# Inner norm moved from VectorE to ScalarE and GpSimd, the last groups normalised in PSUM batch by batch, and a reordered first group, in a two-layer graph kernel

## The chip, the cores and the metric

The kernel runs on one core of one Trainium2 chip. A core has TensorE (PE in the profile; PEld is its weight load), VectorE (DVE), ScalarE (ACT), GpSimd (POOL) and SyncE (SP), which here only issues DMA transfers. The metric is the device time of one execution in microseconds. The time of a version is the median of its runs.

## The reference, cut to what matters

The input x is 128 batches of 128 tokens by 512 features; adj is a 128 x 128 matrix.

```python
A = einsum('od,bdn->bon', adj, x); C = A + b[None, :, None]
pre = A[:, :, None, :] + (C - A)[:, :, :, None]
x = layernorm(x + max(relu(pre), axis=-1))
# layer 1: masked attention with 8 heads, projection, inner norm, residual
q, k, v = split(x @ w_qkv)
attn = softmax(where(adj == 0, -inf, q @ k.T * scale))
o = (attn @ v) @ w_proj + b_proj
ln = (o - mean(o)) * rsqrt(var(o) + 1e-5) * ln_gamma + ln_beta
x = layernorm(x + o + ln)
```

The "inner norm" is `ln`; the outer one is the last line. All data and products are float32.

## The kernel before, in words

**Tiling.** The 128 batches are 32 groups of four. A group passes through layer 0 (`l0_mm`, `l0_stats`, `l0_norm_one`, a transpose through DRAM), then `qk_unit`, `scores`, `softmax`, `v_unit`, `attend`, `o_unit` and `tails`. Three groups are in flight: in turn p of the main loop, group p has its softmax and v, group p+2 its layer 0, group p+1 its q and k, group p-1 its output projection and tail.

**Products.** q and k come from sums of blocks of tokens times 26 ready-made sums of weight blocks (`weight_forms`, tile wqk), with partial results carried between PSUM banks by ScalarE copies into `u` tiles (L777) or other banks (L773). The token sums (`token_sums`, tiles hl) are GpSimd's. v and the output projection use seven products for eight (`Unit`), again with sums on GpSimd.

**First group.** There is no wqk yet, so q and k of group 0 come from plain products (`qk_plain`), which read x1T, transposed on TensorE (`l0_transpose_pe`, L567) and copied from PSUM to SBUF by VectorE (L583). Ahead of that adj is transposed (L422) and copied (L423), layer 0 runs for each batch, and `finish` (L462) makes scale `rs` and shift `sh` on GpSimd for a ScalarE norm (`norm`, L495).

**Tails.** `tails` (L1155) takes statistics of o on VectorE, `rs` on GpSimd (`root_only`, L1144), then two VectorE instructions for each batch: (o - mean) * gamma, then times rs plus o, into z. GpSimd adds z to the reloaded row r (2 batches at once), and a second norm on ScalarE gives the output. z is one buffer for both halves of a group; r lies in xr0 and xr1. r was written to DRAM (`spill`) after GpSimd had added ln_beta to it (`l0_beta_spill`, L591), and only then is the x buffer reloaded for a later group.

**Last groups.** Group 31 has a plain projection for each batch (`project`, L1376). Group 30's tail is `tail_pool` (L1348): a ScalarE norm, then three GpSimd passes. Group 31's is `tail_open` and `tail_close` (L1386, L1406): VectorE as above, with r added in PSUM by a product with the identity. `outer` (L1365) is the second norm and the output.

**Order.** Nothing is issued as the code stands. Each step is `plan.add(engine, cost, emit, reads, writes)`; `Plan.run` (L194) simulates the engines with these costs. TensorE's steps keep their program order. Every other step has a due time worked back from what needs it (`schedule`, L217), and each engine takes the ready step that is due first. A step that nothing needs, such as an output transfer, was due at the end of the whole program plus 9 us. The resulting order is then fixed for every engine and for SP's queue.

Of the kernel before, what the change touches and what calls it, by code (L numbers as in the profile page):

```python
# [135 lines left out]
class Op:  # L136
    __slots__ = ("n", "eng", "cost", "emit", "lag", "kb", "preds", "succs", "due", "start", "done")
# [22 lines left out]
class Plan:  # L160
# [5 lines left out]
    def add(self, eng, cost, emit, reads=(), writes=(), lag=None, kb=0):  # L166
        op = Op(len(self.ops), eng, cost, emit, self.LAG[eng] if lag is None else lag, kb)
        for accesses, writing in ((reads, False), (writes, True)):
# [22 lines left out]
    ROUNDS, KEPT = 4, 0.5  # L191
    SLOWER, LATER = 1.05, 2.0

    def run(self, lead):  # L194
# [10 lines left out]
        for _ in range(self.ROUNDS):  # L205
            order = self.schedule(start)
            last = max(op.done for op in start)
            if best is None or last < best[0]:
                best = last, order
            t = was = lead  # L210
            for op in start:
                t += self.KEPT * (op.start - was)
                was, start[op] = op.done, t
                t += op.cost
        return best[1]

    def schedule(self, ideal):  # L217
        ops = self.ops
        end = max(ideal[op] + op.cost for op in ideal) + 9.0
        for op in reversed(ops):  # L220
            ahead = op.lag + (self.AHEAD_DMA + 1.5 * op.kb / self.KB_PER_US if op.kb else self.AHEAD)
            due = min(
                (s.due - (0.0 if s.eng == op.eng == "PE" else ahead) for s in op.succs),
                default=end,
            )
# [22 lines left out]
        while todo:  # L248
# [16 lines left out]
            op.done = free[e] = now + op.cost * (1.0 if e == "PE" else self.SLOWER)  # L265
# [19 lines left out]
def kernel(  # L285
# [137 lines left out]
    plan.add("DVE", 0.25, lambda: pin(V.tensor_copy(adjT.t, pt0.t[:, :P])), [pt0], [adjT])  # L423
# [33 lines left out]
    def bn(src, reads, mv, c):  # L457
        st = small("st", 6)
        plan.add("DVE", 0.61, lambda: pin(V.bn_stats(st.t, src())), reads, [st])  # L459
        plan.add("DVE", 0.09, lambda: pin(V.bn_aggr(mv.t[:, c], st.t)), [st], [(mv, c)])  # L460
# [33 lines left out]

    def norm(dst, src, stat, reads, writes):  # L495
# [20 lines left out]
    def l0_stats(g):  # L516
        mv = buf(f"mvy{g % 2}", [P, G, 2])
        for j in range(G):
            xb = xs[2 * g + j // 2]
            bn(lambda xb=xb, j=j: xb.t[:, j % 2], [(xb, j % 2)], mv, j)  # L520
# [46 lines left out]
    def l0_transpose_pe(f, k):  # L567
# [5 lines left out]
        def emit():  # L573
            for c in range(KC):
# [4 lines left out]
        plan.add(  # L579
            "DVE",  # L580
            0.61,
            lambda: pin(
                V.tensor_copy(  # L583
                    xT.t[:, h, :, ts(j, P)], b.t.rearrange("p (c n) -> p c n", c=KC)
                )
            ),
            [b],
            [(xT, (h, j))],
        )
# [23 lines left out]
    def weight_forms():  # L613
# [12 lines left out]
        turn = 0  # L626

        def add(dst, dst_at, a, b, sa, sb_):
            nonlocal turn
            (ba, ka, pa), (bb, kb, pb) = a, b  # L630
            reads = [(ba, ka), (bb, kb)]
            if sa < 0 and sb_ < 0:
# [5 lines left out]
                    [dst_at],  # L638
                )
# [4 lines left out]
            turn += 1  # L644
            if turn % 5 < 3:
                plan.add("DVE", 0.62, lambda: tt(V, dst(), pa(), pb(), op), reads, [dst_at])
            else:
                plan.add("POOL", 0.71, lambda: tt(GP, dst(), pa(), pb(), op), reads, [dst_at])
# [38 lines left out]
    def qk_plain(h, banks, eng):  # L687

        xT = x1T_buf(0)
        for n in range(4):  # L690
            b = bank(banks[n])
            for half in range(2):
# [11 lines left out]
                plan.add("PE", 1.725, emit, [raw[n], (xT, (h, 0)), (xT, (h, 1))], [b])  # L704
# [315 lines left out]
    def softmax(b, bs):  # L1020
# [45 lines left out]
        for i in range(H):  # L1066
            plan.add(
                "ACT",
                0.295,
                lambda i=i: pin(  # L1070
                    A.activation(  # L1071
                        flat()[:, i], flat()[:, i], AF.Identity, scale=rec.t[:, i : i + 1]
                    )
                ),
                [rec, (s, i)],
                [(s, i)],
            )
        u = buf(f"pu{b % 2}", [P, Q, H, QS])
# [76 lines left out]
    def tails(g):  # L1155
# [5 lines left out]
        rs = root_only(mv, range(G))  # L1161
        rows = []
        for h in range(2):
# [5 lines left out]
            for j in range(2):  # L1169
                c = 2 * h + j  # L1170
                plan.add(
                    "DVE",
                    0.7,
                    lambda z=z, o=o, j=j, c=c: stt(
                        z.t[:, j], o.t[:, j], mv.t[:, c, 0:1], ga_bc.t, ALU.subtract, ALU.mult
# [308 lines left out]
```

## Time and profile before

| | |
|---|---|
| median of 3 runs | 1913.92 us (1913.4 to 1914.2) |
| profiled execution, its own time | 1916.16 us |
| its span | 1914.4 us |
| granted TensorE clock, mean | 0.994 |
| busy share: PE, DVE, ACT, POOL | 98%, 81%, 73%, 70% |
| mean DMA rate | 179 GB/s |

The span runs from the first to the last instruction of the profiled execution, which is one execution and not the median. Lines of the profile name the line of the code (a helper such as L340, `tt`, or L343, `stt`, stands for many steps, so the tiles tell them apart), the engine, the operation, output and inputs with their shapes. In the list of groups there follow the count, the busy time in us with the mean in ns, and the idle time of the engine ahead of them with what ended it. A matmul of float32 shows as two records.

### The profile page before, as it was taken

Reading aid. Unit: us, or ns where it says so; the run is one execution under the profiler, and the core shown is the slowest. Engines: PE = TensorE matmul, PEld = TensorE weight load, DVE = VectorE, ACT = ScalarE, POOL = GpSimd, SP = SyncE. Lnnn points to the kernel's source line nnn. Section 1 sums busy time; section 2 is a strip of 40 time slices with the busy share of each in tenths; the row PEclk is TensorE's granted clock in tenths of the full one; section 3 lists DMA queues with packets and bytes.
Section 4 is the critical chain, followed back from the end, with each engine's and each line's share of the span. In section 5 each row is a group of like instructions: output and inputs, shape, how many; then the busy total and the mean of one; then the engine's idle time right before and its main releaser. Section 6 shows DMA issues by size and latency. Waiting matters only on the chain.

```text
span 1914.4 us, 35277 instructions
## 1 busy us (share of the span) xinstructions
PE 1876.4 (98%) x11307; PEld 1595.4 (83%) x11307; DVE 1558.2 (81%) x2634; ACT 1405.4 (73%) x4285; POOL 1332.8 (70%) x1454
## 2 busy tenths in 40 slices
PE   9899999999999999999999999999999999999995
PEld 6788888888888888888888888888888888888882
DVE  7678878889788878888788888888788887888774
ACT  2776778777778777778777787776788767787784
POOL 7658667667577767777677767686776776777746
PEclk9999999999999999999999999999999999999998
DMA  6656675566766566765576756676765667666653
GB/s 204 183 130 155 184 204 162 171 168 193 204 188 168 172 179 187 210 178 167 164 194 179 211 164 172 169 200 186 211 144 172 179 188 210 178 170 171 165 193 116
DMA packets 444856, 341.89 MB, mean 179 GB/s; under 512 B 276736, under 2 KB 378240, under 8 KB 444672
## 3 DMA queue, kind: packets, MB, share of 16 engines
q1 hardware_dynamic: 444384, 339.11, 63.7%
q8 instruction: 91, 1.49, 0.3%
q14 instruction: 93, 0.76, 0.1%
q10 hardware_dynamic: 288, 0.52, 0.1%
HBM read 172.82 MB, written 166.72 MB: 177 GB/s over the span
## 4 chain that ended last, share of the span: by engine, by line
PE 91%; DVE 3%; ACT 3%; POOL 1%; issue 1%; DMA 0%; ACTq 0%; DVEq 0%; POOLq 0%
PE k L346 91%; DVE z L343 2%; ACT s L1071 1%; ACT s L1054 1%; POOL x L340 1%; DVE wqk L340 0%; ACT u L777 0%; DVE k L340 0%; POOL rs L340 0%; ACT k L773 0%; DMA x<-in_x_dram 0%; DVE qk L343 0%; ACT x L501 0%; DVE st L459 0%; DVE x1T L583 0%
## 5 line engine op out<-in xcount | busy, mean ns | idle before, releaser
L346 PE MATMUL k<-hl,wqk 128*128 128x256 f32 x2232 | 518.9, 380 | 2.1 <-ACT k L773 2.0
L346 PEld LDWEIGHTS k<-hl,wqk 128*128 128x128 f32 x2232 | 424.4, 190 | 61.2 <-POOL hl L340 2.5
L1054 ACT ACTIVATE s<-s,nm 128x128 f32<-128x128 f32 x1024 | 397.2, 391 | 31.2 <-DVE nm L1045 31.2
L340 POOL TENSOR_TENSOR hl<-x1T 128x512 f32<-128x512 f32 (+1 forms) x250 | 237.8, 961 | 134.3 <-PE k L346 90.2
L1071 ACT ACTIVATE s<-s,rec 128x128 f32<-128x128 f32 x1024 | 325.5, 392 | 0.0
L346 PE MATMUL k<-x1T,wqk 128*128 128x256 f32 x992 | 250.0, 383 | 9.1 <-ACT u L777 5.6
L886 ACT COPY u<-k 128x512 f32<-128x512 f32 x189 | 110.0, 582 | 196.1 <-PE k L346 195.4
L777 ACT COPY u<-k 128x512 f32<-128x512 f32 x341 | 194.2, 584 | 73.2 <-DVE k L340 30.6
L346 PE MATMUL k<-wv,hl 128*128 128x256 f32 x1024 | 241.4, 379 | 0.0
L346 PEld LDWEIGHTS k<-wv,hl 128*128 128x128 f32 x1024 | 194.5, 190 | 52.1 <-issue 21.5
L346 PE MATMUL k<-wp,so 128*128 128x256 f32 x992 | 224.8, 379 | 0.5 <-ACT k L861 0.5
L343 DVE SCALAR_TENSOR_TENSOR s<-k,mask 128x512 f32<-128x512 f32 x256 | 156.2, 683 | 83.0 <-PE k L346 83.0
L346 PEld LDWEIGHTS k<-x1T,wqk 128*128 128x128 f32 x992 | 188.3, 191 | 40.6 <-ACT u L777 11.4
L343 DVE SCALAR_TENSOR_TENSOR qk<-k,u 128x512 f32<-128x512 f32 x248 | 165.4, 682 | 62.9 <-PE k L346 39.9
L346 PEld LDWEIGHTS k<-wp,so 128*128 128x128 f32 x992 | 188.4, 190 | 26.6 <-ACT k L861 0.9
L340 POOL TENSOR_TENSOR hl<-x1T,hl 128x512 f32<-128x512 f32 (+1 forms) x249 | 201.9, 822 | 0.5 <-DMA x1T<-xhop 0.5
L1054 ACT ACTIVATION_READ_ACCUMULATOR s<-s,nm 128x1 f32 x1024 | 194.2, 190 | 0.0
L346 PE MATMUL k<-wv,x1T 128*128 128x256 f32 x768 | 179.5, 383 | 0.0
L340 POOL TENSOR_TENSOR x<-x,be_bc 128x1024 f32<-128x1024 f32 x62 | 153.2, 2470 | 35.1 <-ACT xr L501 16.4
L346 PE MATMUL k<-wp,oT 128*128 128x256 f32 x744 | 170.7, 379 | 0.0
L1083 DVE STREAM_TRANSPOSE pu<-s 128x1024 f32<-128x1024 f32 x128 | 158.1, 1235 | 12.1 <-ACT s L1071 12.0
L1132 ACT COPY oT<-k 128x512 f32<-128x512 f32 x128 | 74.9, 585 | 120.3 <-PE k L346 120.3
(139 smaller groups left out, 3345.1 us busy)
## 6 DMA issues: line engine op xcount, KB each, us to landing
hop<-pu SPq DMA_DIRECT2D x128, 512.0 KB, 2.7
s<-hop SPq DMA_DIRECT2D x512, 128.0 KB, 3.7
spill<-x SPq DMA_DIRECT2D x62, 512.0 KB, 4.3
xhop<-xt SPq DMA_DIRECT2D x248, 128.0 KB, 3.4
x1T<-xhop SPq DMA_DIRECT2D x248, 128.0 KB, 5.0
x<-in_x_dram SPq DMA_DIRECT2D x60, 512.0 KB, 5.9
xr<-spill SPq DMA_DIRECT2D x60, 512.0 KB, 5.4
out_dram<-xr SPq DMA_DIRECT2D x60, 512.0 KB, 4.4
```

The source lines that it names most:

```text
L340: pin(eng.tensor_tensor(dst, a, b, op))
L343: pin(V.scalar_tensor_tensor(dst, a, s, b, op0, op1))
L346: pin(PE.matmul(dst, lhsT=lhsT, rhs=rhs, start=start, stop=True, skip_group_check=True))
L777: plan.add("ACT", 0.5, lambda b=b, u=u: pin(A.copy(u.t, b.t)), [b], [u])
L886: plan.add("ACT", 0.5, lambda: pin(A.copy(u.t, b.t)), [b], [u])
L1054: A.activation(flat()[:, i], flat()[:, i], AF.Exp, bias=nm.t[:, i : i + 1], accum_out=sm.t[:, i : i + 1],)
L1071: A.activation(flat()[:, i], flat()[:, i], AF.Identity, scale=rec.t[:, i : i + 1])
L1083: V.transpose(u.t.rearrange("p q h b -> p h q b"), flat().rearrange("p h (q a) -> p h q a", q=Q),)
L1132: lambda: pin(A.copy(dst.t[:, :, ts(jj, P)], bk.t.rearrange("p (c n) -> p c n", c=KC))),
```

## The change

It has six parts.

1. The planner: a step that nothing needs is due 9 us after the start of the TensorE step ahead of it in the program. Steps marked `both` take VectorE and GpSimd together in the plan. It makes six rounds and not four.
2. First group: the statistics stand behind the copy of adj; `finish_first` makes the shift on VectorE; the copy of x1T is split between VectorE and ScalarE, and a product waits for its half alone; two of the l0 products of group 1 come two plain products later.
3. `weight_forms`: sums that were shared between VectorE and GpSimd are all VectorE's.
4. `softmax`: in group 0 (last two batches) and group 31 (first two) the final scale is one VectorE instruction, not eight ScalarE ones.
5. `tails`: the inner norm is a ScalarE norm and two more GpSimd passes over two batches.
6. Last groups: `tail_before` for group 30 norms into a PSUM bank and then has two VectorE passes, with r + o on GpSimd; `tail` for group 31 works in its PSUM bank. They are called batch by batch between attends and projections; the products with the identity go.

```diff
 class Plan:
+        op.after, op.both = self.pe, both
+        op.preds.update(behind)
-    ROUNDS, KEPT = 4, 0.5
+    ROUNDS, KEPT, BEHIND = 6, 0.5, 9.0
     def schedule(self, ideal):
-        end = max(ideal[op] + op.cost for op in ideal) + 9.0
...
+            if op.succs:
+                due = min(s.due - (0.0 if s.eng == op.eng == "PE" else ahead) for s in op.succs)
+            else:
+                due = ideal.get(op.after, 0.0) + self.BEHIND
...
+            op.done = now + op.cost * (1.0 if e == "PE" else self.SLOWER)
+            if op.both:
+                op.done += max(0.0, free["POOL"] - now)
+                free["POOL"] = op.done
+            free[e] = op.done
+    def finish_first(mv, c, rows):
+        rs, t, sh = small("rs", G), small("st", 6), small("sh", G)
+        def root():
+            pin(GP.tensor_scalar(rs.t[:, :1], mv.t[:, c : c + 1, 1], EPS, None, ALU.add))
+            tt(GP, rs.t[:, :1], rs.t[:, :1], mhalf.t, ALU.pow)
+        plan.add("POOL", 0.85, root, [(mv, c), mhalf], [rs])
+        r = lambda: rows.t[:, c : c + 1]
...
+            lambda: pin(V.tensor_scalar(t.t[:, :1], mv.t[:, c : c + 1, 0], r(), None, ALU.add)),
...
+                V.tensor_scalar(
+                    sh.t[:, :1], r(), t.t[:, :1], rs.t[:, :1], ALU.subtract, ALU.mult
+                )
...
     def l0_stats(g):
-            bn(lambda xb=xb, j=j: xb.t[:, j % 2], [(xb, j % 2)], mv, j)
+            bn(lambda xb=xb, j=j: xb.t[:, j % 2], [(xb, j % 2)], mv, j, [adj_done])
     def l0_transpose_pe(f, k):
+        for half in range(2):
+            at = [(xT, (h, j, half))]
+            if half:
+                plan.add("ACT", 0.4, lambda ops=operands: pin(A.copy(*ops())), [b], at)
+            else:
+                plan.add("DVE", 0.4, lambda ops=operands: pin(V.tensor_copy(*ops())), [b], at)
     def weight_forms():
-            if turn % 5 < 3:
-                plan.add("DVE", 0.62, lambda: tt(V, dst(), pa(), pb(), op), reads, [dst_at])
-            else:
-                plan.add("POOL", 0.71, lambda: tt(GP, dst(), pa(), pb(), op), reads, [dst_at])
+            plan.add("DVE", 0.49, lambda: tt(V, dst(), pa(), pb(), op), reads, [dst_at], both=True)
-    def softmax(b, bs):
+    def softmax(b, bs, on_vector=False):
+        if on_vector:
+                "DVE",
+                1.55,
+                lambda: tt(
+                    V, flat(), flat(), rec.t.unsqueeze(2).to_broadcast([P, H, P]), ALU.mult
+                ),
...
     def tails(g):
-        rs = root_only(mv, range(G))
+        stat = finish(mv, range(G))
...
-                    lambda z=z, o=o, j=j, c=c: stt(
-                        z.t[:, j], o.t[:, j], mv.t[:, c, 0:1], ga_bc.t, ALU.subtract, ALU.mult
-                    ),
...
-                    lambda z=z, o=o, j=j, c=c: stt(
-                        z.t[:, j], z.t[:, j], rs.t[:, c : c + 1], o.t[:, j], ALU.mult, ALU.add
-                    ),
...
+                norm(
+                    lambda z=z, j=j: z.t[:, j],
+                    lambda o=o, j=j: o.t[:, j],
+                    stat[2 * h + j],
+                    [o],
+                    [(z, j)],
                 )
+            plan.add(
+                "POOL",
+                2.34,
+                lambda z=z: tt(GP, z.t, z.t, ga_bc.t.unsqueeze(1).to_broadcast([P, 2, D]), ALU.mult),
+                [z, ga_bc],
+                [z],
+            )
+            plan.add("POOL", 2.34, lambda z=z, o=o: tt(GP, z.t, z.t, o.t, ALU.add), [z, o], [z])
             plan.add("POOL", 2.34, lambda z=z, r=r: tt(GP, r.t, r.t, z.t, ALU.add), [z, r], [r])
...
-        (s,) = finish(mv0, [c], rcol[0])
-        l0_norm_one(0, c, s)
+        l0_norm_one(0, c, finish_first(mv0, c, rcol[0]))
...
-    for f, k in zip(range(4, 8), (0, 1, 2, 3)):
-        l0_mm(f, k)
+    for f in (4, 5):
+        l0_mm(f, f - 4)
...
+    qk_plain(1, (4, 5, 6, 7), copies, range(2))
+    for f in (6, 7):
+        l0_mm(f, f - 4)
+    qk_plain(1, (4, 5, 6, 7), copies, range(2, 4))
...
-            softmax(a + j, bs[j])
+            softmax(a + j, bs[j], p == 0 and j >= 2)
...
+        softmax(a + j, bs[j], j < 2)
-    def tail_pool(b, o, j):
...
+    def tail_before(b, k):
+        bn(lambda: o.t[:, j], [o], mv, 0)
+        plan.add("POOL", 1.25, lambda: tt(GP, r(), r(), o.t[:, j], ALU.add), [rk, o], [rk])
+        (st,) = finish(mv, range(1))
+        pz = bank(k)
+        norm(lambda: pz.t, lambda: o.t[:, j], st, [o], [pz])
+        plan.add("DVE", 0.61, lambda: tt(V, pz.t, pz.t, ga_bc.t, ALU.mult), [pz, ga_bc], [pz])
+        plan.add("DVE", 0.61, lambda: tt(V, z(), pz.t, r(), ALU.add), [pz, rk], [zk])
+        outer(b, zk, z, mz)
+    def tail(b, pb):
+        bn(lambda: pb.t, [pb], mv, 0)
+        rs = root_only(mv, range(1))
+        plan.add("DVE", 0.61, lambda: tt(V, r(), r(), pb.t, ALU.add), [pb, rk], [rk])
...
+            lambda: stt(pb.t, pb.t, mv.t[:, 0, 0:1], ga_bc.t, ALU.subtract, ALU.mult),
...
+            lambda: stt(z(), pb.t, rs.t[:, :1], r(), ALU.mult, ALU.add),
...
+        outer(b, zk, z, mz)
...
-    attend(a + 1, Y[1])
-    for j in range(G):
-        tail_pool(a - G + j, os_[g - 1, j // 2], j % 2)
...
+    for j in range(1, G):
+        attend(a + j, Y[j % 2])
+        tail_before(a - G + j - 1, Y[2 + j % 2])
+        project(a + j - 1, pbs[j - 1])
+        tail(a + j - 1, pbs[j - 1])
+    tail_before(a - 1, Y[2])
     project(a + 3, pbs[3])
+    tail(a + 3, pbs[3])
```

## The prediction, on record before the run

> **What bounds the kernel now.** I read the page's busy shares and its chain first.
>
> ```profile
> PE 1876.4 (98%) x11307; PEld 1595.4 (83%) x11307; DVE 1558.2 (81%) x2634; ACT 1405.4 (73%) x4285; POOL 1332.8 (70%) x1454
> PE 91%; DVE 3%; ACT 3%; POOL 1%; issue 1%; DMA 0%; ACTq 0%; DVEq 0%; POOLq 0%
> ```
>
> TensorE is the bound: 38 us of 1914.4 are without a matmul, and 91% of the chain is matmuls. Everything else matters only where TensorE waits, so the next view is the list of TensorE's waits (us in total, times, longest), and beside it busy time by stage (PE, weight load, DVE, ACT, POOL, clock, DMA).
>
> ```profile
> PE k L346 <- ACT u L777: 5.6, 5, 1.1
> PE k L346 <- ACT k L773: 5.1, 3, 3.1
> PE k L346 <- DMA s<-hop: 1.5, 1, 1.5
> PE k L346 <- ACT u L886: 1.0, 1, 1.0
> ...
> 80.00:100.00 20.00, 15.17 (x56) 12.28 (x56) 10.07 (x14) 13.79 (x32) 7.67 (x5) 0.83 0.74 179
> 160.00:1800.00 1640.00, 1633.81 (x10001) 1401.80 (x9998) 1371.42 (x2313) 1238.26 (x3777) 1157.98 (x1213) 1.00 0.66 181
> 1890.00:1900.00 10.00, 4.83 (x11) 1.63 (x9) 5.33 (x10) 3.04 (x4) 9.25 (x23) 0.91 0.08 29
> 1900.00:1915.00 15.00, 0.00 (x0) 0.00 (x0) 4.29 (x11) 3.74 (x5) 6.66 (x23) 0.50 0.32 120
> ```
>
> The steady state (160 to 1800) loses 6.2 us in all. The rest is lost at the ends: before the first real product, at 81-87, and after the last matmul (1895.8 to 1914.4), where POOL is the busy engine. The start and the end in order of time (start, us, engine):
>
> ```profile
> 5.22 0.69 DVE L459 BATCH_NORM_STATS2 st<-x 128x6 f32<-128x512 f32 x1 [0.81 <-DMA x<-in_x_dram]
> 5.83 0.27 DVE L423 COPY adjT<-k 128x128 f32<-128x128 f32 x1
> 6.16 2.07 PE L346 MATMUL k<-x,adjT 128*128 128x512 f32 x2 [0.99 <-DVE adjT L423]
> ...
> 14.71 1.29 DVE L583 COPY x1T<-k 128x512 f32<-128x512 f32 x2 [0.56 <-PE k L575]
> 16.05 7.17 PE L346 MATMUL k<-x1T,oT 128*128 128x256 f32 x32 [0.94 <-DVE x1T L583]
> ```
>
> The adjacency copy stands behind statistics that wait for x; the first plain product starts at 16.05 behind two x1T copies. Costs of the inner norm and of the nearest forms, from the groups (busy us, mean ns):
>
> ```profile
> L343 DVE SCALAR_TENSOR_TENSOR s<-k,mask 128x512 f32<-128x512 f32 x256 | 156.2, 683 | 83.0 <-PE k L346 83.0
> L343 DVE SCALAR_TENSOR_TENSOR z<-z,rs,o 128x512 f32<-128x512 f32 x120 | 151.9, 1279 | 0.9 <-POOL rs L340 0.9
> L343 DVE SCALAR_TENSOR_TENSOR z<-o,mvo,ga_bc 128x512 f32<-128x512 f32 x120 | 130.0, 1112 | 0.4 <-POOL xr L340 0.4
> L340 POOL TENSOR_TENSOR xr<-xr,z 128x1024 f32<-128x1024 f32 x60 | 141.5, 2358 | 18.5 <-DVE z L343 11.9 <-DMA xr<-spill 6.5
> L501 ACT ACTIVATE x<-x,sh,rs 128x512 f32<-128x512 f32 x128 | 100.5, 809 | 20.1 <-POOL sh L340 20.1
> ```
>
> **What the Trainium skill says.** "SBUF — State Buffer", section "Who interferes with whom": a VectorE instruction with two SBUF inputs and a GpSimd instruction that reads SBUF exclude each other for a whole instruction; with at most one SBUF input it doesn't contend. The trace agrees: the same form takes 683 ns with a PSUM input and 1112 to 1279 with two SBUF inputs. "ScalarE: Activation LUTs", section "What ACT_TABLE_LOAD costs": back-to-back ACTIVATEs overlap by about 93 ns; here two norms of 809 take 1.52 us, 0.71 each extra. "TensorE: Matmul & The Clock Gate", section "What's actually happening": half clock until a window of some 3.4 us was busy. Here the first l0 products are cold (2.07 us a pair, 1.02 from 11.06 on), so an earlier start need not bring the warm clock earlier.
>
> **The change part by part**, against the profiled span of 1914.4.
>
> (1) Adjacency first, first norm partly on DVE, x1T copies split. The transpose of adj ends at 4.31, so adjT can be copied at 4.35 instead of 5.83; the warm-up matmuls hold TensorE to about 4.95, so the first product moves from 6.16 to 5.0: 1.2 us. The shift, three POOL steps from rc at 9.48 to norm at 10.51, becomes two DVE steps of 0.2 us: about 0.3. The two copies (1.29) become half copies of 0.4 us on each of DVE and ACT (the 128x256 rows are 0.41 and 0.40), and a product needs only its half: 0.45. The second batch also loses one 0.68 bn_stats that stands in front of its rc, if the new order avoids it: 0.35. Sum 2.3 (1.0 to 3.5).
>
> (2) Mixed order of qk_plain(1) and l0_mm. TensorE waits 0.86 and 0.90 us at 34.4 and 35.6, for a qk copy and x1T copies that stand on DVE behind weight sums. The last two l0 products now come 7 us later, so the first wait goes; the second may stay in part, since only one pair of products (1.7 us) covers the copies. 1.3 (0 to 1.8). The weight sums all go to DVE: 14 fewer POOL sums of 0.73-1.04 (11 us), 14 more on DVE at 0.41 alone or about 1.4 behind a POOL instruction. They are hidden because wqk is first read at 69.06; DVE is 36.7 of 40 us busy at 10 to 50, so that cover is thin, and without it TensorE waits at 69. Cost 0 (0 to 3).
>
> (3) Softmax scale of two batches on DVE in group 0. Between 70 and 87 ACT never rests and TensorE waits 1.76 + 3.07 = 4.83 us for bank copies behind it. Sixteen scales of 0.305 (2.44 for 8) leave ACT: 4.9. In their place DVE has two 128x1024 multiplies: 1.2 each by the 1197 ns reduce over as many elements, at most 3.6 behind a 2.36 us POOL instruction. DVE is idle for over 10 us there. Gain 4.3 (3 to 4.8).
>
> (4) Inner norm in `tails`, 30 groups. Off DVE: 4 x (1.28 + 1.11) = 9.6 us a group. Onto ACT: 4 x 0.72 = 2.9. Onto POOL: 4 x 2.36 + 0.32 + 0.20 = 10.0. Five groups of 58 us read apart show a mean of DVE 47.4, ACT 43.2, POOL 39.7: they become 38, 46, 50 of 58. None passes TensorE. What it can buy is the 5.6 us wait for `u` (five times 1.1): the chain there is two z (2.87), z (1.76), `k` add, `u` copy, so the long z instructions are the cause, and they go. The new due times (9 us behind the last TensorE instruction in front) also pull the tail early, ahead of other POOL work. Gain 2.0, from +5 to a loss with no firm bound (below).
>
> (5) Last groups. In the last softmax, scales of two batches leave ACT (4.9 us), which was in one run of work from 1850 to 1868.6; of TensorE's waits of 0.5 and 1.0 I credit 1.0. From the attend at t0 (1869.11 before) the tail lasted 45.3 us. POOL had 3 passes of 1.27 for each of four batches and its roots, 31 us from 1870 on. Two passes of each go (10 us), and so do the four identity products (8 records, 4.3 us) with their 0.94 wait. After: TensorE needs 4 attends x 1.03 + 1.92 + 4 projections x 3.63 = 20.6, with the 1.5 us DMA wait gone since the last softmax is earlier. DVE gets more: per earlier batch two PSUM passes of 0.69, per last batch one. Its list, overlaps taken off: 3 results 1.9, four times 2.7, four times 3.45, in all 26.5, with some 1.6 idle at first, so its last statistics end near t0 + 28. Then root, shift and hops 1.3, norm 0.81, output and end 2.9 (1911.5 to 1914.4): t0 + 33.2, and 2 for an order that isn't perfect: 35.2. TensorE's own path, 20.6 + 9.5 for the last batch, is shorter, so DVE takes over from POOL. Gain 10.1 + 1.0 = 11.1 (6 to 15). The norm into PSUM is taken at 0.81; at 0.7 nothing changes.
>
> Sum: 2.3 + 1.3 + 4.3 + 2.0 + 11.1 = 21.0, so a span of 1893.4. The profiled execution took 1916.2 around its span of 1914.4 while the runs' median is 1913.9, 0.5 below that span: **1893 us**.
>
> **The rivals.** *Forecast*, 0.55: 1887 to 1899. *Some of it given back in the steady state*, 0.22: POOL at 86% and ACT norms among bank copies make TensorE wait 0.4 us a group, 12 us: 1905 (1899 to 1912). For it: POOL waits 95.6 us for TensorE's release of hl, so its work is not free to move; against: over 8 us a group stay idle, and no TensorE wait is on POOL now. *End not shorter*, 0.10: DVE and POOL take turns, 3 of the 10 us are won: 1900. *Slower*, 0.13: x is reloaded only after POOL's x+be. In one steady group x+be runs at 907.6, the load is issued at 918.6, takes 6.4 us, and TensorE reads x at 926.6: 1.6 us in hand. If two tail passes (4.7 us) are put in front of it, TensorE waits 3.1 us in each of 29 groups: 1893 + 90 + 2 = 1985; one pass (2.4 us) already costs 22 us, and there it decides. Against it: due times count the reload, so the planner can put x+be first.
>
> A difference under 0.2% (3.8 us) can't be told from none. Faster: the first three and nothing else, less a little that ends within 3.8: 0.84; same 0.03; slower 0.13. The range leaves out the slower case (0.13) and 0.05 below: 1886 to 1912.
>
> **What would show it.** (1) First plain product near 13.7. (2) No waits at 34-36. (3) No ACT wait at 81-87. (4) POOL 84-88% and DVE 65-68% in the steady state, no `u` wait, and attends 57.8 us apart; a wait of TensorE on x, hl or ACT there makes me wrong. (5) Last matmul to end about 12 us, DVE and not POOL in the chain at the end.

## The result, and the profile after

The changed kernel takes **1890.5 us** (median of 4 runs, 1889.5 to 1890.8) beside 1914.1 for the kernel before on the same chip: a ratio of 0.9876 [0.9859, 0.9894], 23.6 us less. Run again with other kernels later it took 1889.1 (ratio 0.9866 [0.9853, 0.9879]). The forecast was 1893, 1886 to 1912. The profiled execution has a span of 1887.7, against 1914.4 before: 26.7 us less, 3.1 more than the medians say. The profiled execution of before was 2.1 us slower than its median (1916.16 for 1914.06), and the one of after 1.0 us faster (1889.46 for 1890.48). All readings of stages below are of these two executions and add up to the 26.7.

First the page's busy shares and the shares of its chain, after the change:

```profile
PE 1865.2 (99%) x11299; PEld 1592.8 (84%) x11299; DVE 1328.0 (70%) x2432; ACT 1484.1 (79%) x4377; POOL 1543.4 (82%) x1600
PE 96%; ACT 1%; POOL 1%; DVE 1%; issue 0%; DMA 0%; SPq 0%; POOLq 0%; ACTq 0%
```

DVE falls from 1558.2 to 1328.0 us, POOL rises from 1332.8 to 1543.4 and ACT from 1405.4 to 1484.1. TensorE has 22.5 us without a matmul where it had 38.0. Its busy time falls as well, by 11.2 us: the four identity products are gone (eight records), and there are fewer short stalls and slow stretches that the profile counts as busy (below). Next the list of TensorE's waits after (us in total, times, longest):

```profile
PE k L353 <- ACT k L806: 2.8, 2, 1.4
PE k L353 <- ACT u L810: 1.6, 1, 1.6
...
PE k L353 <- DVE x1T L627: 1.0, 1, 1.0
```

The five waits on `u` of before, all of them in the steady state, are gone. The one of 1.6 belongs to group 0 (at 84.19), as does one of the two waits on `k` (at 78.89; the other is at 1810.69). Then busy time by stage (PE, weight load, DVE, ACT, POOL, clock, DMA), first after, in the stages that were shown of before and at the end:

```profile
80.00:100.00 20.00, 18.22 (x177) 15.84 (x176) 16.97 (x24) 9.41 (x17) 14.42 (x10) 1.00 0.89 230
160.00:1800.00 1640.00, 1640.00 (x9974) 1410.87 (x9973) 1146.32 (x2100) 1334.63 (x3948) 1382.70 (x1396) 1.00 0.66 181
1862.00:1872.00 10.00, 9.02 (x34) 3.97 (x34) 10.00 (x22) 4.40 (x7) 7.58 (x22) 1.00 0.33 100
1872.00:1882.00 10.00, 1.97 (x5) 0.57 (x3) 9.18 (x20) 2.44 (x3) 7.26 (x21) 0.79 0.21 79
```

and the stretch of before that answers to the third of them, ten to twenty us after the last group's first attend:

```profile
1879.00:1889.00 10.00, 8.47 (x34) 4.02 (x33) 3.29 (x7) 2.44 (x4) 9.98 (x10) 1.00 0.41 118
```

In the steady state TensorE is busy for the whole of 1640 us; DVE has 70% there and POOL 84%. At the end POOL was the full engine (9.98 of 10, DVE 3.29); after the change it is DVE (10.00 and 9.18 of 10).

Two fixed points serve for the rest: the first plain product, and the starts of the attends of each group, whose distance is TensorE's true period. In us from the span's start:

| | before | after | gained since the row above |
|---|---|---|---|
| first plain product | 16.05 | 14.28 | 1.8 |
| first scores of group 0 | 49.65 | 46.41 | 1.5 |
| first attend of group 0 | 100.28 | 92.15 | 4.9 |
| first attend of group 1 | 158.12 | 150.54 | -0.5 |
| first attend of group 29 | 1782.47 | 1765.38 | 9.5 |
| first attend of the last group | 1869.11 | 1852.24 | -0.2 |
| end of span | 1914.4 | 1887.7 | 9.8 |

From group 1 to group 29 the attends after are 57.67 us apart without exception but one of 57.84. Before, 14 of these 28 periods were 57.67, five were 59.06, and the other nine lay between 57.74 and 58.06. The timeline of the start after (start, us, engine) answers to the one of before:

```profile
4.35 0.29 DVE L430 COPY adjT<-k 128x128 f32<-128x128 f32 x1 [3.23 <-PE k L429]
4.56 1.41 DVE L466 BATCH_NORM_STATS2 st<-x 128x6 f32<-128x512 f32 x2
...
4.96 1.91 PE L353 MATMUL k<-x,adjT 128*128 128x512 f32 x2
```

The statistics now stand behind the adjacency copy, and the first product behind the warm-up starts at 4.96 where it was 6.16. And the groups of the inner norm after (busy us, mean ns):

```profile
L347 POOL TENSOR_TENSOR z<-z,ga_bc 128x1024 f32<-128x1024 f32 x60 | 142.0, 2366 | 29.1 <-ACT z L537 29.1
L347 POOL TENSOR_TENSOR z<-z,o 128x1024 f32<-128x1024 f32 x60 | 141.9, 2365 | 1.6
L537 ACT ACTIVATE z<-o,sh,rs 128x512 f32<-128x512 f32 x120 | 94.2, 813 | 3.1 <-POOL xr L347 3.1
L347 DVE TENSOR_TENSOR k<-k,ga_bc 128x512 f32<-128x512 f32 x4 | 2.7, 680 | 0.0
```

They cost what the rows of before said: 2366 and 2365 on POOL for a forecast of 2.36 us, 813 on ACT for 809, 680 in PSUM for 0.69.

### The profile page after: what moved, and what is told of

It reads as the page before. It is cut to its first block, busy times and chain, and to the rows that moved or that the text cites. A ratio compares the mean times of both kernels' runs of the same rounds, so it can differ in the third digit from the quotient of the medians.

```text
span 1887.7 us, 35406 instructions
## 1 busy us (share of the span) xinstructions
PE 1865.2 (99%) x11299; PEld 1592.8 (84%) x11299; DVE 1328.0 (70%) x2432; ACT 1484.1 (79%) x4377; POOL 1543.4 (82%) x1600
## 4 chain that ended last, share of the span: by engine, by line
PE 96%; ACT 1%; POOL 1%; DVE 1%; issue 0%; DMA 0%; SPq 0%; POOLq 0%; ACTq 0%
PE k L353 96%; ACT s L1116 0%; ACT s L1087 0%; POOL rs L347 0%; DVE st L466 0%; ACT k L806 0%; DMA s<-hop 0%; SPq L357 0%; POOL x L347 0%; POOL hl L347 0%; ACT z L537 0%; POOL rs L478 0%; ACT u L810 0%; POOL sh L486 0%; DVE pu L1128 0%
## 5 line engine op out<-in xcount | busy, mean ns | idle before, releaser
L1116 ACT ACTIVATE s<-s,rec 128x128 f32<-128x128 f32 x992 | 312.5, 392 | 0.0
L347 POOL TENSOR_TENSOR hl<-x1T 128x512 f32<-128x512 f32 (+1 forms) x250 | 216.6, 874 | 81.4 <-PE k L353 73.1
L353 PE MATMUL k<-x1T,wqk 128*128 128x256 f32 x992 | 244.8, 379 | 3.0 <-ACT u L810 1.6
L350 DVE SCALAR_TENSOR_TENSOR qk<-k,u 128x512 f32<-128x512 f32 x248 | 169.9, 688 | 109.5 <-PE k L353 73.4
L347 POOL TENSOR_TENSOR hl<-x1T,hl 128x512 f32<-128x512 f32 (+1 forms) x249 | 197.5, 807 | 0.2 <-DMA x1T<-xhop 0.2
L347 POOL TENSOR_TENSOR x<-x,be_bc 128x1024 f32<-128x1024 f32 x62 | 146.4, 2361 | 46.4 <-DVE xt L572 27.2
L347 POOL TENSOR_TENSOR z<-z,ga_bc 128x1024 f32<-128x1024 f32 x60 | 142.0, 2366 | 29.1 <-ACT z L537 29.1
```

What stands on the lines that cost most here:

```text
L347: pin(eng.tensor_tensor(dst, a, b, op))
L350: pin(V.scalar_tensor_tensor(dst, a, s, b, op0, op1))
L353: pin(PE.matmul(dst, lhsT=lhsT, rhs=rhs, start=start, stop=True, skip_group_check=True))
L1116: A.activation(flat()[:, i], flat()[:, i], AF.Identity, scale=rec.t[:, i : i + 1])
```

## The experiments

The order of all instructions is written by a planner, which keeps the best of several trial orders. Most edits make it choose another order, and then two things have changed. So the first eight experiments, which undo, do or vary one part, are followed by three in which the order is **held**: the edit leaves what the planner is told as it is, and changes only which engine runs an instruction, or what it copies. In the traces of these three, VectorE, ScalarE and GpSimd run the same sequence as in the changed kernel, the moved instructions apart. But the planner doesn't know what was moved, so their place in the new queue is not one that it would choose. The first attend of the last group, "t0", stands beside the times.

### One part undone or done alone, planned anew

**The inner norm of the 30 tails back on DVE.**

```diff
-                norm(z, o, stat)                     # ScalarE
-            plan.add("POOL", ... z * ga_bc); plan.add("POOL", ... z + o)
+                plan.add("DVE", 0.7, ... stt(z, o, mean, ga_bc, subtract, mult))
+                plan.add("DVE", 0.7, ... stt(z, z, rs, o, mult, add))
```

> The changed kernel with its tails of groups 0 to 29 as before (two VectorE instructions a batch, none of the two extra GpSimd passes); all else as changed. Theory (long z instructions on VectorE delay the bank add and the u copy): the steady state goes back to stalls, 9.5 us lost between the first and the thirtieth attend, some 1899 to 1901 us. Rival (the new due times took the stalls away, whatever engine does the norm): attends stay 57.67 us apart, 1890 to 1892 us.

Measured: 1947.9 us (1945.8 to 1950.9), ratio 1.0183 [1.0166, 1.02]; t0 at 1907.70. Nearly all attends are 59.67 us apart. TensorE's waits there, and the second pass:

```profile
PE k L353 <- ACT u L810: 48.0, 28, 1.9
```

```profile
L350 DVE SCALAR_TENSOR_TENSOR z<-z,rs,o 128x512 f32<-128x512 f32 x120 | 174.7, 1476 | 0.9 <-POOL rs L347 0.9
```

The miss is large: 28 waits for `u` instead of five (one of them that of group 0), and a second pass of 1476 ns instead of 1279. The part undone is worth more than the whole change, so something in the rest of the change made the old passes worse than they were before. The suspects are the new due times and the planner not knowing that these passes hold GpSimd up.

**The same, with the planner told that both passes wait for GpSimd and hold it.**

```diff
+                    both=True,
```

> Tails as before on VectorE inside the changed kernel, as in the run with the old tails, but both z instructions are marked as taking the shared port, so that the plan counts them on GpSimd too; nothing else changes. Theory (that run lost 57 us because the plan counts a z instruction at 0.7 us, puts it ahead of a bank add by its early due time, and on the chip it takes up to 2.3 us behind GpSimd): with the wait in the plan attends come within 57.7 to 58.3 us of each other and the time is 1888 to 1905 us. Rival (the early due time alone forces the z instructions ahead of the bank add, whatever the plan knows): 59 us and more a group, 1930 us or more.

Measured: 1909.4 us (1907.2 to 1913.1), ratio 0.997 [0.9957, 0.9983]; t0 at 1872.05. 38.5 of the 57 us are gone by telling the planner alone. (A pass behind GpSimd took up to 2.86 us in the run before, not 2.3.) So they were the price of an order made in ignorance, not of the passes. It still lies 19 us above the changed kernel, 4 us above the range expected, with 7.4 us of waits on `u` and 5.3 on reloads of x.

**The kernel before with the new tails and nothing else.**

```diff
-    def tails(g): ...      # as before
+    def tails(g): ...      # as after
```

> The kernel before with nothing but the new tails of groups 0 to 29 (one ScalarE norm a batch, two more GpSimd passes for two batches), with the old due times and planner. Theory: the steady state alone gains its 9 to 10 us, 1904 to 1906 us. Rival (it needs the new due times or the planner's view of the shared port): less than 4 us gained or a loss, 1910 us or more.

Measured: 1907.2 us (1904.7 to 1908.7), ratio 0.9964 [0.9951, 0.9977]; t0 at 1860.05, t0 to end 45.5. No period of 59.06 is left. Between the first attends of groups 1 and 29 there are 1617.9 us where before had 1624.4: 6.4 gained, although two periods of 59.0 come in, each with a wait for a reload of x of 1.1 us. Without those two it would be about 9.0 (6.4 + 2 x 1.32), near what the whole change gained there; but they belong to the order chosen for this kernel, and the time is 1.2 us above the range expected.

**Instructions without a successor due at the program's end again, not 9 us behind the last TensorE instruction in front.**

```diff
-                due = ideal.get(op.after, 0.0) + self.BEHIND
+                due = end
```

> The changed kernel with the due time of steps that nothing needs put back to the end of the program plus 9 us; all else as changed. Theory (z off VectorE is what counts): attends stay within 0.1 us of 57.67 apart, and at most 2 us change, at the end, 1889 to 1893 us. Rival (due times made the gain): 5 to 10 us of stalls return, 1896 to 1900 us.

Measured: 1894.4 us (1894.0 to 1895.1), ratio 0.9899 [0.9884, 0.9914]. Attends 57.67 apart throughout, t0 at 1851.09; t0 to end 41.6 instead of 35.5. That is 3.9 us in the time, where at most 2 were expected, and 6 us from t0 to the end; TensorE started sooner here. With the old due times the outer norms of four batches are put off to the end: GpSimd makes their roots one after another between 1882.45 and 1886.64, and ScalarE's last norms follow. In the changed kernel the roots lie between the other steps. In the steady state the due times do nothing.

**The due times pulled earlier by 15 us**, meant to put tail passes ahead of other POOL work as the slower rival had it.

```diff
-    ROUNDS, KEPT, BEHIND = 6, 0.5, 9.0
+    ROUNDS, KEPT, BEHIND = 6, 0.5, -6.0
```

> The changed kernel with the due time of steps that nothing needs 15 us earlier (6 us ahead of the last TensorE step in front, not 9 behind); no instruction differs. The slower rival of the prediction (tail passes ahead of the ln_beta sum hold up the reload of x): TensorE waits for x, 0.5 us a group or more, 1905 us or more. Theory (GpSimd keeps over 8 us a group free and the due times of the reload keep the sum ahead): attends stay 57.67 us apart, 1886 to 1894 us.

Measured: 1894.7 us (1893.2 to 1896.3), ratio 0.9892 [0.9877, 0.9907]; attends 57.67 apart, t0 at 1855.05, t0 to end 36.3. One wait for x, 0.9 us, between groups 0 and 1. The edit didn't bring about the rival's order, though. In one group the tail passes start 3 us earlier (896.82 for 899.95), but GpSimd's sequence is the same in all groups of both kernels: two sums of x and ln_beta, then the three passes of one half, then those of the other. So the rival's case was not tested.

**One trial order only.**

```diff
-    ROUNDS, KEPT, BEHIND = 6, 0.5, 9.0
+    ROUNDS, KEPT, BEHIND = 1, 0.5, 9.0
```

> The changed kernel with one round of planning, so that the order of round 0 is used and not that of round 3; no instruction differs. Theory (what the starts of other runs differ by is the round that was picked, since the run with the old last groups used round 0 and reached its first attend 1.4 us and its second 2.2 us earlier): attends 1 and 2 near 90.7 and 148.4 us, group 30 near 54.4 us, the end unchanged at 35 to 37 us after its first attend, 1885 to 1888 us. Rival (the new last groups themselves changed the start, or round 0 is worse at the end): 1889 us or more.

Measured: 1901.3 us (1899.2 to 1903.3), ratio 0.9923 [0.9906, 0.9939]; t0 at 1865.16. TensorE's longest item in the list of waits there:

```profile
PE k L353 <- DMA x<-in_x_dram: 7.6, 5, 2.3
```

The choice of the order alone is worth some 9 to 11 us (by the ratios, or by the times), and the expectation (1885 to 1888) was wrong. In that order three consecutive groups late in the program took 58.87, 61.75 and 59.82. The reload of x has so little in hand that an order can uncover it. In one group read in both, the second load was issued at 905.09 and read at 914.62 in the changed kernel, 9.5 us later; with one trial order at 909.06 and 916.11, 7.1 us later. But it isn't the slower rival's mechanism: up to the last group GpSimd's sequence of sums and tail passes is the same in both orders. At one of the stalls (TensorE resumes at 1554.26) the sum had ended at 1535.10 and the load was issued 13.4 us later, at 1548.53, behind other transfers in SP's queue. At the same place of the changed kernel 11.3 us passed (1529.98 to 1541.29), and the load stood 7.8 us ahead of its matmul where 3.6 were left here. The expectation also says that the changed kernel uses the order of round 3, the fourth; if so, four rounds would have found it as well, and the step to six does nothing.

**The softmax scale of two batches in group 0 back on ACT.**

```diff
-            softmax(a + j, bs[j], p == 0 and j >= 2)
+            softmax(a + j, bs[j], False)
```

> The changed kernel with the softmax scale of group 0 back on ScalarE; all else as changed. Theory (16 scales of 0.305 us were what TensorE waited behind at 81 to 87 us): the span from the scores of group 0 to the first attend grows from 45.7 to 49.5 to 50.6 us, 1893 to 1896 us. Rival (VectorE's weight sums or the order of the copies limit that stretch now): less than 2 us, 1889 to 1892 us.

Measured: 1908.4 us (1904.6 to 1913.4), ratio 0.9965 [0.9954, 0.9976]; t0 at 1870.81. From the scores of group 0 to its first attend it takes 51.58 us (46.27 to 97.85), against 45.74 in the changed kernel and 50.63 before: 5.8 us back, 1 more than was expected. The other 13 come later: this order has attends up to 59.33 apart and eight waits for x, 6.2 us listed. Of this run only the part up to 97.85 tells anything on the softmax scale.

**The last groups as before.**

```diff
-    for j in range(1, G): attend; tail_before; project; tail
+    attend; for j in range(G): tail_pool; project; ...      # as before
```

> The changed kernel with the last two groups as before (three GpSimd passes for each batch of group 30, identity products for group 31); all else as changed. Theory (GpSimd passes and roots in a row made the end long): about 45 us from the last group's first attend to the end where the changed kernel has 35.5, so 9 to 11 us more, 1900 to 1902 us. Rival (the relief of ScalarE in the last softmax and the due times shortened the end): at most 4 us more, up to 1894 us.

Measured: 1895.1 us (1894.0 to 1895.6), ratio 0.9901 [0.9887, 0.9916]. t0 to end is 44.94 instead of 35.46: 9.5 us, nearly the old end (45.29 before). But t0 is at 1848.56, 3.7 us earlier than in the changed kernel, because another order was chosen and TensorE warmed up sooner (below). So undoing this part costs 9.5 and shows only 4.6 in the time.

### The chip or the order

The changed kernel once more, among the held runs.

> The changed kernel once more, to tell a chip from an order. r1, u_soft0 and u_tails_port had TensorE waits of 6 to 8 us for reloads of x that the changed kernel did not show in its first run. If these come with the order that the planner chose for those kernels, this run again gives 1889 to 1892 with attends 57.67 us apart and no wait on DMA. If they come from the chip that the second set of runs fell on, waits on x appear here too on a chip of that kind, and the time is 1893 to 1905.

Measured: 1889.1 us (1889.1 to 1889.5), ratio 0.9866 [0.9853, 0.9879]; t0 at 1852.00, no wait for x. This doesn't separate the two causes, since the run fell on the chip of the first set, while three of the four kernels with waits for x of 2 to 8 us in all (`u_tails_port`, `r1`, `u_soft0`) ran on another. What the other runs show: on that other chip the kernel with earlier due times has only one such wait, of 0.9, and on the first chip the kernel before with new tails has two of 1.1. So the chip alone doesn't make the waits, and the order matters; whether the chip adds to them stays open.

### With the order held

**DVE's two passes in the tails, in the order of the changed kernel.** The first pass runs where ACT's norm stood, the second where POOL's multiply stood, and POOL's add is gone.

```diff
-                norm(z, o, stat)
+                plan.add("ACT", 0.7, ... stt(z, o, mean, ga_bc, subtract, mult))   # issued to VectorE
-            plan.add("POOL", 2.34, ... tt(GP, z, z, ga_bc, mult))
-            plan.add("POOL", 2.34, ... tt(GP, z, z, o, add))
+            plan.add("POOL", 2.34, ... stt(z, z, rs, o, mult, add))                # issued to VectorE
+            plan.add("POOL", 2.34, lambda: None)
```

> The order of the changed kernel held fixed; only the inner norm of the 30 tails is done by VectorE's two passes per batch again, the first in the place of ScalarE's norm, the second in the place of GpSimd's multiply, and GpSimd's add is gone. It separates what the passes cost from what the planner makes of them (the old tails planned anew took 57 us). Theory (the passes themselves, with their lock against GpSimd, delay the chain of bank add and u copy): VectorE back at 47 of 58 us a group, TensorE waits on u of 0.3 to 1.4 in some or all groups, 8 to 45 us in all: 1898 to 1935. Rival (only the order was worth something): attends stay 57.67 apart, 1889 to 1892.

Measured: 1912.5 us (1910.3 to 1916.4), ratio 0.9989 [0.9982, 0.9995], 23.3 above the changed kernel in the same set. From group 1 to group 29 it takes 1637.6 us where the changed kernel took 1614.8; the end is the same, and the start 1.1 us earlier, since TensorE warmed up sooner (below). TensorE's waits in just that stretch, and the two passes:

```profile
PE k L353 <- DVE v L347: 5.1, 10, 1.3
PE k L353 <- DVE rec L1098: 5.1, 6, 1.3
```

```profile
L350 DVE SCALAR_TENSOR_TENSOR z<-o,mvo,ga_bc 128x512 f32<-128x512 f32 x120 | 129.8, 1085 | 0.0
...
L350 DVE SCALAR_TENSOR_TENSOR z<-z,rs,o 128x512 f32<-128x512 f32 x120 | 99.8, 870 | 0.0
```

The passes cost TensorE 22.8 us in this order although they run faster than before (870 and 1085 ns). TensorE now waits for other VectorE work that stands behind them, and hardly for `u`. So the passes themselves are a cause, and not only the order. Where they hurt, and how much, depends on the order: between groups 1 and 29 there are 9.5 us more than after in the order of before, 22.8 here, 15.8 where the planner knew that they hold GpSimd (some of it waits for x), and 54.3 where it didn't. Here, too, the planner didn't know of the passes on VectorE, so the 22.8 are no price of the passes in a good order. Of these 22.8 us the list of waits holds 11.6 (with 0.8 on `u` and 0.6 on `hl` in two more lines).

**Two of five weight sums on GpSimd again.**

```diff
+            e = V if turn % 5 < 3 else GP
-            plan.add("DVE", 0.49, lambda: tt(V, dst(), pa(), pb(), op), ..., both=True)
+            plan.add("DVE", 0.49, lambda: tt(e, dst(), pa(), pb(), op), ..., both=True)
```

> The order of the changed kernel held fixed; only where it runs differs for two of every five weight sums: GpSimd again, as before, in the place that the plan gave them on VectorE. Theory (weight sums cost nothing, as step 2 said): scores and first attend within 0.5 us of 46.4 and 92.2, time within 2 us of the changed kernel. Rival (the sums on VectorE were part of what stops the 1.4 and 1.6 us waits at 77 to 84 from going): first attend 1 to 3 us earlier. On the other side, a POOL sum of 0.73 to 1.04 us before hl could make the first attend up to 2 us later.

Measured: 1889.5 us (1888.5 to 1890.0), ratio 0.9866 [0.9851, 0.9881]; scores at 46.17, first attend at 91.92, and the waits of 1.4 and 1.6 us at 77 to 84 as they were. In this order it makes no difference where these sums run.

**An attempt at better: the other half copied first, and two batches' passes to POOL.**

```diff
-            def operands(half=half):
+            def operands(half=half ^ (f == 1)):
...
+        if b < a - 2:
+            norm(z, o, st)
+            plan.add("DVE", 0.61, ... tt(GP, z, z, ga_bc, mult))     # issued to GpSimd
+            plan.add("DVE", 0.61, ... tt(GP, z, z, r, add))          # issued to GpSimd
```

> An attempt at better, with the order of the changed kernel held fixed. (a) In the first group the half of x1T that the first plain product needs is the one that ScalarE copies first for the second batch: first plain product at about 13.85 instead of 14.28, if the 0.99 us wait is VectorE's copy standing behind ScalarE's copy of the same bank; if it is the transposes, no change. (b) In the last groups the two batches a-4 and a-3 have their multiply and add on GpSimd in SBUF (1.27 us each) instead of VectorE in PSUM (4 x 0.68 = 2.7 us), VectorE being 27 of 30 us busy. Theory (VectorE's list sets the end): last attend group to end 35.5 becomes 33 to 34.7, together 1887 to 1889.5. Rival (the roots on GpSimd are on the path too, so its 5 us of passes delay them): 35.5 to 37, 1890 to 1892.

Measured: 1893.2 us (1892.5 to 1896.9), ratio 0.9891 [0.9877, 0.9904]: slower than the changed kernel by 4. The first half works. The timelines of the first group, after and then here:

```profile
12.81 0.37 ACT L625 COPY x1T<-k 128x256 f32<-128x256 f32 x1 [0.24 <-DVE x1T L627]
...
13.40 0.36 ACT L625 COPY x1T<-k 128x256 f32<-128x256 f32 x1
...
13.80 0.42 DVE L627 COPY x1T<-k 128x256 f32<-128x256 f32 x1 [0.31 <-ACT x1T L625]
...
14.28 1.99 PE L353 MATMUL k<-x1T,oT 128*128 128x256 f32 x8 [0.99 <-DVE x1T L627]
```

```profile
12.84 0.36 ACT L625 COPY x1T<-k 128x256 f32<-128x256 f32 x1
13.23 0.42 DVE L627 COPY x1T<-k 128x256 f32<-128x256 f32 x1 [0.31 <-ACT x1T L625]
...
13.25 1.99 PE L353 MATMUL k<-x1T,oT 128*128 128x256 f32 x8 [0.53 <-ACT x1T L625]
```

In both, the two half copies of one bank never run together: each is released by the other engine's. So the product starts 0.46 us sooner behind its transposes if the half that it needs is the one copied first (a wait of 0.53 for 0.99); the rest of the step from 14.28 to 13.25 is the warm-up (below). The second half of the edit fails. t0 is at 1851.09, but t0 to end is 40.9 instead of 35.5, beyond both ranges expected. What DVE waits for in the last groups:

```profile
DVE st L466 <- POOL x L347: 5.7, 2, 3.0
```

Taking 2.7 us off the busy engine added 5.7 of waiting to it: its next statistics, in a fixed place in its queue, wait for POOL passes that themselves stand behind roots, and TensorE then stands 5.3 us for an `oT` copy. The changed kernel, which has these passes on DVE in PSUM, has no such wait in its list for these groups. No run beat the changed kernel; the first half of this edit alone was not tried.

## Why the prediction was right

The time was near: 1890.5 for 1893. But the terms were worked out against the profiled span, and there they make 21.0 where 26.7 were measured: one term was small by 7.5 us, and all other misses together were 1.8 the other way. That the time was only 2.5 us off is partly luck, since 3.1 of the 26.7 us lie in which executions were profiled.

**(1) Start, 2.3: measured 1.8.** The adjacency copy came at 4.35 and the first product at 4.96, as worked out. The split of the x1T copies bought nothing: TensorE waited 0.99 us behind them where it waited 0.94 before. The step had let the two halves run at once, 0.45 us saved. The Trainium skill ("PSUM — Partial Sum Buffer", section "PSUM bank collisions raise a hardware error") says that two engines must not be in the same bank and 32-partition quadrant at once, reads against reads included, and that the software has to keep them apart. The trace fits this: each half copy starts when the other engine's has released it. Another part is not the kernel's: the first product pair took 1.91 us in the profiled run, but in the same order elsewhere 1.03, by when TensorE's clock warmed up, and the first plain product lies at 14.28 in the one and 13.11 in the other. The gains of the two executions, 1.8 and 2.9, have the step's 2.3 between them. The norm's own part (0.3 and 0.35) was not tested alone.

**(2) Mixed order, 1.3: measured 1.5.** No wait at 34 to 36 is left. That the weight sums cost 0 is shown for this order: with it held, moving two of five back changes nothing. The new place of the two l0 products was not undone alone.

**(3) Softmax scale in group 0, 4.3: measured 4.9 in the table, and 5.8 where it was taken back.** But "no ACT wait at 81 to 87" was wrong: 1.39 us at 78.89 and 1.61 at 84.19 remain, behind exponentials and bank copies on ACT. By the lists only 4.83 - 3.00 = 1.8 us of waiting went, while the stretch is 4.9 shorter. Most of the rest is the clock, which the step left out. The first lines are of before, the next of after, the last of the run with the scale back on ACT:

```profile
86.96 2.08 PE L346 MATMUL k<-x1T,wqk 128*128 128x256 f32 x4 [3.07 <-ACT k L773]
88.83 1.91 PE L346 MATMUL k<-hl,wqk 128*128 128x256 f32 x4
```

```profile
84.19 1.13 PE L353 MATMUL k<-x1T,wqk 128*128 128x256 f32 x4 [1.61 <-ACT u L810]
```

```profile
85.72 2.08 PE L353 MATMUL k<-x1T,wqk 128*128 128x256 f32 x4 [4.81 <-ACT k L806]
```

Behind the wait of 3.07 the same four records take 2.08 us instead of 1.13; the granted clock was 0.50 from 88 to 92, while after the change it was 1.00 throughout. From the first record behind that wait to the first attend before needed 13.3 us; the same records took 10.7 after, the wait of 1.61 left out. So 1.8 us are waits, 2.6 the clock, and some 0.4 are in neither. With the scale back on ACT the waits (7.07 us) and the slow clock (0.51 from 82 to 86) came back. The size came out near because the clock made up for the waits that stayed.

**(4) Tails, 2.0: measured 9.5. This is the term that was mis-sized.** The shares were near (DVE 70% for 65 to 68, POOL 84% for 84 to 88; the page of before priced each pass), no wait for `u` was left in the steady state, and the passes of DVE were the cause, as the chain through one stall of before says (start, us, what; by the profile TensorE has no matmul from 845.26 to 846.38):

```profile
839.86 2.87 DVE z L343 x2
...
843.34 1.76 DVE z L343
845.10 0.62 DVE k L340
...
845.74 0.60 ACT u L777
```

The held run shows it by putting them back, and the kernel before with new tails alone by taking them out: its 59.06 periods are gone. What failed is the step that took the 5.6 us of listed `u` waits as all that could be won, and credited part of that. The periods of before hold 1624.4 us where 28 of 57.67 make 1614.8: 9.6 us lost, of which the list shows 5.6 on `u` and 0.2 on another. In the held run it shows 11.6 of 22.8, in the first experiment 46.9 of 54.3 (1669.1 from group 1 to group 29). TensorE's records around the stall, before, show what is missing:

```profile
843.36 1.03 PE L346 MATMUL k<-hl,wqk 128*128 128x256 f32 x4
844.23 1.03 PE L346 MATMUL k<-x1T,wqk 128*128 128x256 f32 x4
846.38 1.13 PE L346 MATMUL k<-x1T,wqk 128*128 128x256 f32 x4 [1.13 <-ACT u L777]
847.35 1.03 PE L346 MATMUL k<-hl,wqk 128*128 128x256 f32 x4
```

Four records start 0.87 us after the four ahead of them when nothing stalls. Here the starts are 2.15 and then 0.97 apart, 1.39 us lost in all, as the period of 59.06 says; the list counts 1.13, from the modelled end of the record ahead, which lies behind the moment at which the next could have started. One group later the two steps at this place (from 903.29) take 2.05 us for 1.73 behind the same `u` copy, a loss of 0.32, and the list shows nothing. So the five stalls hold 7.0 us, and the other 2.7 are in nine periods with stalls too short to be listed, one of 0.2 apart. The period from attend to attend was in the trace before, and would have given 9.6.

**(5) Last groups, 11.1: 10.1 of it for t0 to end, measured 9.8 (35.5 for 35.2), and 9.5 where the old end was put back.** DVE took over from POOL as said; its last statistics end at t0 + 29.5 for t0 + 28, inside the 2 us left for an order that isn't perfect. Of the 1.0 us credited for ACT waits ahead of t0 nothing was left: from group 30 to t0 1.1 us were gained (31.89 to 30.81), but from group 29 to 30 1.3 were lost (54.74 to 56.06), with a wait of 1.37 for ACT at 1810.69 that before doesn't have. Not foreseen was that the new due times carry 6 of the 9.8: with the old ones t0 to end is 41.6. Alone, with the last groups as before, they give 0.4 (44.94), so the gain needs both.

**The rivals.** Nothing was given back in the steady state: 0.4 us a group would have shown as periods of 58.1. The slower one did not come true, and no run put tail passes ahead of the sums in the steady state, so its mechanism stays untested. That the reload of x has little in hand was right: four other orders of almost the same kernel show waits for x of 2 to 8 us, but in a few groups, not in 29, and in the one looked into the load stood late in SP's queue.

## What to carry to other kernels

Size a periodic stall by the period: the distance between two like instructions of the bounding engine, group by group, against its shortest value. A list of waits, which here held between a half and nine tenths of the loss, names the cause but not the amount; and a long wait can cost more than its length, if the clock falls behind it. Where an order is planned, hold the order when you test one part, or the test measures another order too; and before work is moved off a full engine, see what stands next in its queue and whether that will now wait.

## What the runs showed of the hardware that was not expected

- The clock's warm-up is not at a fixed place in the program. The Trainium skill ("TensorE: Matmul & The Clock Gate", section "What's actually happening") says that the window runs on freely and doesn't reset when a kernel starts, so that the warm-up varies by some 500 ns to either side; the traces fit this. In one and the same order, with the first product at 4.96 in each, the first pair of 128x512 products took 1.91, 1.62 and 1.03 us, and the first plain product moved by up to 1.2 us with it. No edit under 1 us in the start can be judged from one profile.
- A VectorE pass over two SBUF operands had means of 870, 1279 and 1476 ns in three orders of the same instruction. The trace of before shows why. Of the 240 passes of the inner norm, 115 start while no GpSimd instruction runs, and take 0.74 us (median). The other 125 start while one runs, and end 0.55 us (median) after that one's end. In the stall above GpSimd's instruction ends at 844.55 and the pass, begun at 843.34, at 845.10. Three other runs with these passes show the same 0.55. So a pass that starts behind a GpSimd instruction takes what is left of that instruction and 0.55 us.
- In this program half copies of one PSUM bank on two engines take turns: 0.36 and then 0.42 us, 0.03 apart, 0.81 for a bank where whole copies took 1.29 for two on one engine. What they would do without the wait between them, no run shows.
- A wait can halve TensorE's clock for some microseconds, and its length alone doesn't decide. Behind waits of 3.07 us (before), 4.81 (softmax scale back), 4.87 (last groups as before) and 5.32 (the attempt at better) records took twice their time. Behind most waits of 1.4 to 2.3 us they did not. But they did behind one of 2.17 (at 1554.26 with one trial order), and behind one of 1.66 that followed closely on one of 1.24 (at 1827.72 with the planner told).
